# Four transformer layers on one core: layers 0 to 2 as one instruction sequence with one set of buffers

## The chip, the cores and the metric

The kernel runs on one core of a Trainium2 chip. Its engines work side by side, each through its own list of instructions, strictly in order: TensorE (PE, matrix products and transposes, with its weight loads shown as PEld), VectorE (DVE), ScalarE (ACT), GpSimd (POOL) and SyncE (SP, which here only issues DMAs). An instruction waits for semaphores that others raise, and whatever stands behind it on its engine waits too. The metric is the device time of one execution in microseconds; lower is better. The kernel before takes 1860.44 us, the median of three runs (1860.05 to 1869.56).

## The reference

The input x is 128 batches of 64 tokens with 128 channels, with a context of the same shape and one condition vector for each batch. Four layers follow one another:

```
L0: x = x + g_sa * (attend(ln(x)*(1+sc_sa)+sh_sa) @ sa_proj_w + b)     16 heads of 8
    x = x + attend(q from ln(x), k and v from context) @ ca_proj_w + b
    x = x + g_ff * (gelu((ln(x)*(1+sc_ff)+sh_ff) @ fc1_w + b1) @ fc2_w + b2)
L1: x = x + attend(q from ada_ln(x), k and v from ada_ln(context)) @ Wp + bp
L2: like L0, with ln(context) for its keys and values
L3: nx = layer_norm(x); evidence = softmax(nx Wq (ctx Wk)^T / sqrt(128)) ctx Wv
    combined = [nx, evidence, condition]
    x = x + sigmoid(gate(combined)) * (sum over 3 experts, by a softmax router, @ out_w + out_b)
```

The shifts, scales and gates of L0, L1 and L2 are products of silu(condition) with weights: small tables that are computed once. All is float32.

## The kernel before

The 8192 tokens are 16 groups of 512 (8 batches), and x stays in on-chip memory throughout (`xs`, one tile a group). The kernel is a row of stages, each a loop over the groups.

**Attention 1** is one pipeline of 32 items: L0's self-attention of 16 groups, then L0's cross-attention of 16. Each item is prepared in eight parts (`prepare`, L294): load of the context, statistics, norm, the transposed key and query inputs, `kT` and its masked copy `kbd` (L342, POOL), `qT`, and the values, written into one of two tiles `vbds`. Then come scores in two halves (`scores`, L365: maximum L382 and subtraction L384 on DVE), transposes and the exponential (`turned`, L390), the product with the values (`weighted`, L406), and `finish` (L427) in four parts: A sends the softmax sums to DRAM and back (L435 to L443); B takes reciprocals on DVE and sends them through DRAM into `rb`, spread over the rows (L445 to L457); C multiplies to `oT` and adds the bias to x on POOL (L460, L462); D projects on PE (`py`, L466) and adds to x on DVE. `attend` (L474) writes the order out by hand: first 8, 5, 3 and 2 parts of items 0 to 3, then steps k, two for an item, in which the parts of neighbouring items alternate. The last steps hold only finishes. For the last two items little else stands between the parts.

**Tables of later layers** (`later_layers`, L204): ten modulations, a folded column, a gate table that goes to DRAM, and two folded rows; each is one product on PE and one or two operations on DVE.

**MLP 0** (`mlp_loop`, L571): turn j holds the norm of group j+2 (POOL), the four hidden products of group j (`hidden`, L584, with Gelu on ACT, L585), the four output products of group j-1 (`output`, L590), the transposes and modulation of group j+1 (`enter`: DVE L258, POOL L259), the statistics of group j+3, the gate of j-1 and the residual of j-2 (`leave`, L602, L603). In each turn stands one group of `measure_context`: a load of the context and its statistics, with some POOL operations (L566 to L569), for the norms of L1 and L2.

**Attention 2** is the same pipeline over 48 items (L1 cross, L2 self, L2 cross). **Layer 3's setup** (L661 to L773) then loads its expert weights and multiplies weights with one another, each time a product on PE and a copy on DVE with two PSUM tiles. **MLP 2** follows, then **layer 3**.

Each of these stages opens its own pools of on-chip buffers and closes them at its end, so that the first loads of a stage wait for the end of the one before. The attention pools hold, in banks of PSUM, two `mm`, one `sc` of four and one `pt` of two; the MLP's hold three `mm`, three `ph` and two `py`. The order of the start (conditions, modulations, tables) is left to the scheduler; within the loops it is as written.

Of the kernel before, what the change touches and what calls it, by code (L numbers as in the profile page):

```python
# [59 lines left out]
def tile_kernel(ctx: ExitStack, tc: tile.TileContext, a: dict, out: bass.AP):  # L60
# [60 lines left out]


    masked = ExitStack()
    mp = masked.enter_context(tc.tile_pool(name="mp", bufs=1))
    dp = ctx.enter_context(tc.tile_pool(name="dp", bufs=1, space=bass.MemoryType.DRAM))
    vbds = []
    for i in range(2):
        t = mp.tile([P, NB, 8, 32], F32, tag=f"vbd{i}", name=f"vbd{i}")
        G.memset(t, 0.0)
        G.memset(t[0:L, :, :, 16:17], 1.0)  # L130
        G.memset(t[L:P, :, :, 17:18], 1.0)
        vbds.append(t)
# [14 lines left out]
    def modulations(ps0, *which):  # L147
        for wname, bname, n, scales in which:
            m = const([P, n, P], "mod_" + wname)
            for i in range(n):  # L150
                pm = ps0.tile([P, 512], F32, tag="ps", name="pm")
                T.matmul(pm[:, :P], w[wname][:, 0, ts(i, P)], scT, start=True, stop=True)
                r = _ROW[bname] + i
                b = (vec1 if i in scales else vec)[:, r : r + 1]
                V.tensor_scalar_add(m[:, i, :], pm[:, :P], b)
            mods[wname] = m
# [3 lines left out]
    def folded_column(ps0, wp, bp, bv, i):  # L160
        pb = ps0.tile([P, 512], F32, tag="ps", name="pb")
        T.matmul(pb[:, 0:1], w[wp][:, 0], col(bv, i), start=True, stop=True)
        t = const([P, 1], "pb_" + wp)
        V.tensor_add(t, pb[:, 0:1], col(bp))
        proj_bias[wp] = t
# [3 lines left out]
    def gate_table(ps0, wmod, wp):  # L169

        table = dp.tile([2, P, P], F32, tag="gate_" + wp, name="gate_" + wp)
        rows = const([P, 2, P], "gate_rows")
        gb = const([P, P], "gate_bias")
        V.tensor_scalar_mul(gb, mods[wmod][:, 2, :], proj_bias[wp])
        for i, src in enumerate((mods[wmod][:, 2, :], gb)):
            pg = ps0.tile([P, 512], F32, tag="ps", name="pg")
            T.transpose(pg[:, :P], src, ident)
            V.tensor_copy(rows[:, i, :], pg[:, :P])
        nc.sync.dma_start(table.rearrange("i b c -> b i c"), rows)
        gates[wp] = table  # L180

    def folded_row(ps0, wp, bp, bv):
        bvs = const([P, P], "bvs")
        V.tensor_copy(bvs, col(bv, 1).broadcast_to([P, P]))
        pb = ps0.tile([P, 512], F32, tag="ps", name="pb")
# [4 lines left out]
    with tc.tile_pool(name="ps0", bufs=2, space=PSUM) as ps0:  # L190
        pc = ps0.tile([P, 512], F32, tag="ps", name="pc")
# [3 lines left out]
        pv = ps0.tile([P, 512], F32, tag="ps", name="pv")  # L195
# [3 lines left out]
        modulations(ps0, ("L0_xcond_adaln_w", "L0_xcond_adaln_b", 6, (1, 4)))  # L199
        folded_column(ps0, "L0_xcond_sa_proj_w", "L0_xcond_sa_proj_b", "L0_xcond_qkv_b", 2)  # L200
        gate_table(ps0, "L0_xcond_adaln_w", "L0_xcond_sa_proj_w")
        folded_row(ps0, "L0_xcond_ca_proj_w", "L0_xcond_ca_proj_b", "L0_xcond_kv_b")

    def later_layers():  # L204
        with tc.tile_pool(name="ps0", bufs=4, space=PSUM) as ps0:
            modulations(
                ps0,
                ("L1_xcond_Wss_q", "L1_xcond_bss_q", 2, (0,)),
                ("L1_xcond_Wss_kv", "L1_xcond_bss_kv", 2, (0,)),
                ("L2_xcond_W_mod", "L2_xcond_b_mod", 6, (1, 4)),  # L210
            )
            folded_column(ps0, "L2_xcond_W_proj", "L2_xcond_b_proj", "L2_xcond_b_qkv", 2)
            gate_table(ps0, "L2_xcond_W_mod", "L2_xcond_W_proj")
            folded_row(ps0, "L1_xcond_Wp", "L1_xcond_bp", "L1_xcond_bkv")
            folded_row(ps0, "L2_xcond_W_cproj", "L2_xcond_b_cproj", "L2_xcond_b_kvc")
# [78 lines left out]
    def prepare(pools, at):  # L294
# [12 lines left out]
        if cross:  # L307
            cn = c
            if layer != "L0c":
                cn = pool.tile([P, TT, P], F32, tag="cn", name="cn")  # L310
# [116 lines left out]
    def finish(pools, at):  # L427
# [20 lines left out]
        rb = pool.tile([P, NT], F32, tag="rb", name="rb")  # L448
# [10 lines left out]
        oT = pool.tile([P, NT], F32, tag="oT", name="oT")  # L459
# [14 lines left out]
    def attend(pools, ats):  # L474
# [9 lines left out]
        for i, parts in enumerate((8, 5, 3, 2)):  # L484
            for _ in range(parts):
                go(prep, i)

        halves = [dict(at=at, u=u) for at in ats for u in range(2)]
        for k in range(2 * n + 6):
# [30 lines left out]

    def attention_of(s, layer):
# [29 lines left out]
    def mlp(wmod, w1, b1, w2, b2, beside=None):  # L551
        with ExitStack() as stack:
            pool = stack.enter_context(tc.tile_pool(name="wk", bufs=2))
            psum = stack.enter_context(tc.tile_pool(name="mm", bufs=3, space=PSUM))
            ph_pool = stack.enter_context(tc.tile_pool(name="ph", bufs=3, space=PSUM))
            py_pool = stack.enter_context(tc.tile_pool(name="py", bufs=2, space=PSUM))
            with tc.manual_schedule():
                mlp_loop(pool, psum, ph_pool, py_pool, wmod, w1, b1, w2, b2, beside)

    def measure_context(pool, s):  # L560
# [10 lines left out]
    def mlp_loop(pool, psum, ph_pool, py_pool, wmod, w1, b1, w2, b2, beside):  # L571
# [6 lines left out]
        def enter(d):  # L578
            d["xm"] = modulated(pool, transposed(psum, d["xn"]), wmod, 4, 3, d["s"])
            d["h"] = pool.tile([P, 4, NT], F32, tag="h", name="h")  # L580

        def hidden(d, f):
            ph = ph_pool.tile([P, 512], F32, tag="ph", name="ph")
# [3 lines left out]
        def output(d, f):  # L587
            if f == 0:
                d["py"] = py_pool.tile([P, 512], F32, tag="py", name="py")
# [21 lines left out]
        go(measure, 0)  # L611
        go(norm, 0)
        go(measure, 1)
        for j in range(-1, NST + 2):
# [9 lines left out]
            if beside and 0 <= j < NST:  # L624
                beside(pool, j)
# [5 lines left out]
    def attention_pools(stack):  # L631
        pool = stack.enter_context(tc.tile_pool(name="wk", bufs=2))
        psum = stack.enter_context(tc.tile_pool(name="mm", bufs=2, space=PSUM))
        psc = stack.enter_context(tc.tile_pool(name="sc", bufs=1, space=PSUM))
        ppt = stack.enter_context(tc.tile_pool(name="pt", bufs=1, space=PSUM))
        return pool, psum, psc, ppt
# [3 lines left out]

    with ExitStack() as stack:
        pools = attention_pools(stack)
        with tc.manual_schedule():
            attend(pools, [attention_of(s, layer) for layer in ("L0s", "L0c") for s in groups])
    later_layers()
    mlp(
        "L0_xcond_adaln_w", "L0_xcond_fc1_w", "L0_xcond_fc1_b", "L0_xcond_fc2_w", "L0_xcond_fc2_b",
        measure_context,
    )


    with ExitStack() as stack:
        pools = attention_pools(stack)
        with tc.manual_schedule():
            attend(
                pools, [attention_of(s, layer) for layer in ("L1c", "L2s", "L2c") for s in groups]
            )
    masked.close()


    keep = ctx.enter_context(tc.tile_pool(name="keep", bufs=1))  # L661
    load_weights("L3_xcond_e", keep)

    def kept(shape, name):
        return keep.tile(shape, F32, tag=name, name=name)

    g_b2 = kept([P, P], "g_b2")
    r = _ROW["L3_xcond_gate_b2"]
    nc.scalar.dma_start(g_b2, a["vecs"][r : r + 1, :].broadcast_to([P, P]))
    out_b = kept([1, P], "out_b")  # L670
    r = _ROW["L3_xcond_out_b"]
    nc.scalar.dma_start(out_b, a["vecs"][r : r + 1, :])

    r_b = kept([P, 1], "r_b")
    V.memset(r_b, 0.0)
    for t in range(TT):
        nc.scalar.dma_start(
            r_b[32 * t : 32 * t + 3, :], a["L3_xcond_router_b"].rearrange("(n o) -> n o", o=1)
        )
    three = kept([1, TT, 32], "three")  # L680
    V.memset(three, 0.0)
    V.memset(three[:, :, 0:3], 1.0)
    b2p = kept([P, TT, 32], "b2p")
    V.memset(b2p, 0.0)
    rw = kept([P, 3, 32], "rw")
    V.memset(rw, 0.0)
    V.tensor_copy(rw[:, 0, 0:3], w["L3_xcond_router_W"][:, 0, :])
    V.tensor_copy(rw[:, 2, 0:3], w["L3_xcond_router_W"][:, 2, :])
    w_qk = kept([P, P], "w_qk")
    w_ev = kept([P, 3, 256], "w_ev")  # L690
    w_gev = kept([P, P], "w_gev")
    w_2o = kept([P, 6, P], "w_2o")

    b_2o = kept([P, TT, P], "b_2o")
    V.memset(b_2o, 0.0)
    ab = kept([P, 7, P], "ab")
    ra = kept([P, NST, 2], "ra")
    pds, prs = [], []
    for i in range(2):
        t = kept([P, TT, P], f"pd{i}")  # L700
        G.memset(t, 0.0)
        pds.append(t)
        t = kept([P, TT, 32], f"pr{i}")
        G.memset(t, 0.0)
# [322 lines left out]
```

## Time and profile before

| view | row | value |
|---|---|---|
| runs | median of 3 | 1860.44 us |
| profiled execution | time, span | 1859.64, 1857.8 us |
| engines | PE busy | 1660.1 us (89%) |
| | DVE, ACT, POOL busy | 1250.0, 1082.8, 1031.6 us |
| timeline | first scores of attention 1 | 32.08 us |
| | last subtraction (L384) of attention 1 ends | 432.01 |
| | first hidden product of MLP 0 | 468.17 |
| | last hidden product of MLP 0 starts | 588.6 |
| | first scores of attention 2 | 614.11 |
| | last subtraction of attention 2 ends | 1234.75 |
| | layer 3's setup: first load issued | 1258.37 |
| | first hidden product of MLP 2 | 1291.62 |
| | last hidden product of MLP 2 starts | 1412.1 |
| DMA | share of the 16 engines, main queue | 17.9% |

The times in the table of the timeline are counted from the start of the span. A busy time is that of an engine's instructions; it says nothing of which engine the others wait for. In the lists of instructions the bracket at the end of a line gives how long the engine was idle before it, and on what it waited.

### The profile page before, as it was taken

What the parts mean: (1) busy time and instruction counts of PE and PEld (TensorE: products, weight loads), DVE (VectorE), ACT (ScalarE), POOL (GpSimd) and SP (SyncE); (2) the same over time, 40 slices, a digit from 0 to 9 for tenths busy, and PEclk for the clock granted to TensorE, in tenths of its full rate; (3) what the DMA queues carried; (4) which work ended last, traced back from release to release, by engine and by line L of the source; (5) the groups of instructions that cost most, each with busy time, mean ns of one, the idle gap of its engine ahead of it and who ended that gap; (6) DMA issues with size and microseconds to landing.
All of it is one profiled execution on the core that took longest, in us unless ns stands there. A gap on an engine that the chain in (4) does not pass through costs nothing.

```text
span 1857.8 us, 64728 instructions
## 1 busy us (share of the span) xinstructions
PE 1660.1 (89%) x27756; PEld 1103.7 (59%) x27756; DVE 1250.0 (67%) x2299; ACT 1082.8 (58%) x1862; POOL 1031.6 (56%) x1665
## 2 busy tenths in 40 slices
PE   5999889995998888899998899966997999999998
PEld 3666667764444566666666667753444566656665
DVE  4899889984453688899898899853342445444544
ACT  3877667772333787778777788841332444444443
POOL 5677777652996666666777667623552232223311
PEclk9999999998999899999999999985997999999999
DMA  6233332212111022212333322111000000000000
GB/s 185 57 86 89 93 94 68 68 45 59 30 34 34 24 58 55 53 44 60 79 89 89 103 68 68 51 51 36 1 1 17 23 18 18 24 23 24 18 7 17
DMA packets 149870, 95.79 MB, mean 52 GB/s; under 512 B 35221, under 2 KB 132431, under 8 KB 149583
## 3 DMA queue, kind: packets, MB, share of 16 engines
q1 hardware_dynamic: 148624, 91.35, 17.9%
q8 instruction: 218, 3.57, 0.8%
q14 instruction: 69, 0.57, 0.1%
q10 hardware_dynamic: 959, 0.30, 0.1%
HBM read 71.41 MB, written 9.70 MB: 44 GB/s over the span
## 4 chain that ended last, share of the span: by engine, by line
PE 55%; DMA 11%; DVE 10%; POOL 8%; issue 6%; ACT 5%; SPq 5%; POOLq 0%; ACTq 0%; DVEq 0%
PE ph L584 6%; PE py L590 6%; PE ph L904 5%; PE ph L905 5%; PE sc L375 5%; PE psT L253 5%; PE pp L400 4%; PE po L417 4%; DMA recs<-rc 3%; PE py L466 3%; DVE e L384 2%; DVE mx L382 2%; PE pk L334 2%; DMA rb<-recs 2%; PE pq L347 2%
## 5 line engine op out<-in xcount | busy, mean ns | idle before, releaser
L382 DVE TENSOR_REDUCE mx<-sc 128x32 f32<-128x2048 f32 x160 | 366.1, 2288 | 80.1 <-PE sc L375 80.0
L404 ACT ACTIVATE eT<-pp 128x1024 f32<-128x1024 f32 x320 | 330.3, 1032 | 103.2 <-PE pp L400 103.2
L384 DVE TENSOR_TENSOR e<-sc,mx 128x2048 f32<-128x2048 f32 x160 | 366.6, 2292 | 5.5
L400 PEld LDWEIGHTS pp<-ident,e 64*128 64x128 f32 x5120 | 184.8, 139 | 201.5 <-issue 80.4
L342 POOL TENSOR_SCALAR kbd<-kT,mask 128x512 f32<-128x512 f32 x320 | 216.1, 694 | 73.3 <-ACT kT L336 73.2
L400 PE MATMUL pp<-ident,e 64*128 64x64 f32 x5120 | 228.7, 229 | 20.7 <-ACT eT L404 15.6
L282 POOL TENSOR_SCALAR xn<-x,nmu,rs 128x128 f32<-128x128 f32 x512 | 223.5, 451 | 13.4
L375 PE MATMUL sc<-kbd,qT 32*64 32x256 f32 x5120 | 181.8, 391 | 23.3 <-DVE e L384 22.8
L460 POOL TENSOR_TENSOR oT<-o,rb 128x512 f32<-128x512 f32 x80 | 102.0, 1275 | 161.9 <-DMA rb<-recs 79.3
L585 ACT ACTIVATE h<-ph,vec 128x512 f32<-128x512 f32 x128 | 88.0, 688 | 173.2 <-PE ph L584 173.2
L907 DVE TENSOR_TENSOR h<-ph,ab 128x512 f32<-128x512 f32 x112 | 77.5, 692 | 157.0 <-PE ph L905 157.0
L417 PE MATMUL po<-eT,vbd 128*32 128x64 f32 x10240 | 177.0, 221 | 1.8 <-ACT eT L404 1.8
L240 POOL TENSOR_SCALAR rs<-mv 128x4 f32<-128x4 f32 x128 | 25.5, 199 | 246.1 <-DVE mv L233 202.4
L417 PEld LDWEIGHTS po<-eT,vbd 128*32 128x32 f32 x10240 | 150.7, 110 | 12.9 <-ACT eT L404 2.1
L241 POOL TENSOR_TENSOR rs<-rs,nhalf 128x4 f32<-128x4 f32 x128 | 130.3, 1018 | 10.7
L911 ACT ACTIVATE h<-h 128x512 f32<-128x512 f32 x112 | 70.4, 630 | 109.0 <-DVE h L907 90.1
L375 PEld LDWEIGHTS sc<-kbd,qT 32*64 32x64 f32 x5120 | 98.9, 132 | 58.9 <-issue 39.4
L336 ACT ACTIVATE kT<-pk,vec 128x512 f32<-128x512 f32 x80 | 55.1, 688 | 109.9 <-PE pk L334 109.9
L231 DVE BATCH_NORM_STATS2 st<-x 128x6 f32<-128x128 f32 x512 | 110.5, 278 | 8.4 <-DMA x<-in_x_dram 8.4
L936 PE MATMUL po<-w_2o,h 128*128 128x128 f32 x768 | 98.5, 278 | 19.1 <-DVE acc L946 18.4
L425 ACT COPY o<-po 128x512 f32<-128x512 f32 x160 | 95.6, 598 | 26.3 <-DMA gt<-gate_L_xcond_W_proj 6.2
L936 PEld LDWEIGHTS po<-w_2o,h 128*128 128x128 f32 x768 | 90.7, 192 | 24.8 <-issue 13.1
(259 smaller groups left out, 2997.2 us busy)
## 6 DMA issues: line engine op xcount, KB each, us to landing
rb<-recs SPq DMA_DIRECT2D x80, 256.0 KB
c<-in_ctx_dram SPq DMA_DIRECT2D x80, 256.0 KB
o<-o SPq DMA_DIRECT2D x320, 32.0 KB
gt<-gate_L_xcond_sa_proj_w SPq DMA_DIRECT2D x64, 128.0 KB
gt<-gate_L_xcond_W_proj SPq DMA_DIRECT2D x64, 128.0 KB
sums<-o SPq DMA_DIRECT2D x320, 8.0 KB
x<-in_x_dram SPq DMA_DIRECT2D x16, 256.0 KB
out_dram<-acc SPq DMA_DIRECT2D x16, 256.0 KB
```

What stands on the lines that cost most here:

```text
L241: G.tensor_tensor(rs, rs, nhalf, ALU.pow)
L282: G.tensor_scalar(xn[:, t, :], src[:, t, :], nmu[:, t : t + 1], rs[:, t : t + 1], ALU.add, ALU.mult)
L342: G.tensor_scalar(kbd[:, j], by_batch(kT), mask[:, j : j + 1], 1.0, ALU.mult, ALU.mult)
L375: T.matmul(sc[ts(h, L), g, ts(t2, 256)], qT[ts(g, 32), ts(b, L)], kbd[ts(g, 32), :, b, :], start=True, stop=True,)
L382: V.tensor_reduce(mx, sc.rearrange("p g (m k) -> p (g m) k", k=L), AX.X, ALU.max)
L384: V.tensor_tensor(e, sc.rearrange("p g (m k) -> p (g m) k", k=L), mx.unsqueeze(2).broadcast_to([P, 32, L]), ALU.subtract,)
L400: T.transpose(pp[:, h, ts(4 * g2 + 2 * i + t2, L)], e6[ts(h, L), 2 * gg + g2, t2, i], ident[ts(h, L), ts(h, L)],)
L404: S.activation(eT[:, gg], pp, AF.Exp, scale=HD ** -0.5)
L417: T.matmul(po[ts(g, 32), i, ts(2 * t2 + h, L)], at["vbd"][:, 4 * u + 2 * t2 + h, 2 * g + i, :], e7[:, g // 2, h, g % 2, i, t2, :], start=T ...
L584: T.matmul(ph, w[w1][:, 0, ts(f, P)], d["xm"], start=True, stop=True)
L590: T.matmul(d["py"], w[w2][:, f, :], d["h"][:, f, :], start=f == 0, stop=f == 3)
L936: T.matmul(po[:, ex, :], d[q][:, ts(t, P)], w_2o[:, q, :], start=r == 0, stop=r == 1)
```

## The change

Layers 0 to 2 become one sequence, written by hand from the first transposes on, with one set of pools (the attention's). `attend` and `mlp` no longer run their loops; they return lists of functions, and `stages` calls these in turn. The tail of an attention (its last four steps) alternates with the head of the MLP's loop (its first four turns, -1 to 2), and the last two turns of MLP 0 alternate with the three functions that prepare the first items of attention 2. The tables of later layers stand one by one in turns 0 to 8 of MLP 0, and layer 3's setup in turns 0 (loads and memsets) and 3 to 15 of MLP 2, joined into fewer PSUM tiles and copies. At the start, only two of L0's six modulations stand ahead of the first scores. `rb`, `oT` and `cn` have one buffer instead of two, the MLP's hidden tile takes the place of `e`, `ph` that of `sc` and `py` that of `pt`, and layer 3's kept tiles take the places of weights that are no longer needed. Layer 3's loop is the same.

```diff
+    pools = (
+        stack.enter_context(tc.tile_pool(name="wk", bufs=2)),
+        stack.enter_context(tc.tile_pool(name="mm", bufs=2, space=PSUM)),
+        stack.enter_context(tc.tile_pool(name="sc", bufs=1, space=PSUM)),
+        stack.enter_context(tc.tile_pool(name="pt", bufs=1, space=PSUM)),
+    )
...
-    def modulations(ps0, *which):
+    def modulations(wname, bname, n, scales):
+        def part(which):
+            pm = mm("pm")
+            for j, i in enumerate(which):
+                T.matmul(pm[:, ts(j, P)], w[wname][:, 0, ts(i, P)], scT, start=True, stop=True)
+            for j, i in enumerate(which):
...
+                V.tensor_scalar_add(mods[wname][:, i, :], pm[:, ts(j, P)], b)
+        return [lambda q=q: part(range(q, min(q + 2, n))) for q in range(0, n, 2)]
...
+    later_tables = [
+        *modulations("L1_xcond_Wss_kv", "L1_xcond_bss_kv", 2, (0,)),
+        *modulations("L1_xcond_Wss_q", "L1_xcond_bss_q", 2, (0,)),
+        *modulations("L2_xcond_W_mod", "L2_xcond_b_mod", 6, (1, 4)),
+        lambda: folded_row("L1_xcond_Wp", "L1_xcond_bp", "L1_xcond_bkv"),
+        lambda: folded_column("L2_xcond_W_proj", "L2_xcond_b_proj", "L2_xcond_b_qkv", 2),
+        lambda: gate_table("L2_xcond_W_mod", "L2_xcond_W_proj"),
+        lambda: folded_row("L2_xcond_W_cproj", "L2_xcond_b_cproj", "L2_xcond_b_kvc"),
+    ]
...
-                cn = pool.tile([P, TT, P], F32, tag="cn", name="cn")
+                cn = pool.tile([P, TT, P], F32, tag="cn", name="cn", bufs=1)
-        rb = pool.tile([P, NT], F32, tag="rb", name="rb")
+        rb = pool.tile([P, NT], F32, tag="rb", name="rb", bufs=1)
-        oT = pool.tile([P, NT], F32, tag="oT", name="oT")
+        oT = pool.tile([P, NT], F32, tag="oT", name="oT", bufs=1)
...
-        for i, parts in enumerate((8, 5, 3, 2)):
-            for _ in range(parts):
-                go(prep, i)
+        heads = [
+            lambda: ahead(0, 1, 2, 0, 1, 0, 1),
+            lambda: ahead(0, 0, 0, 0, 0),
+            lambda: ahead(2, 1, 1, 2, 3, 3),
+        ]
...
+        return heads, [lambda k=k: step(k) for k in range(2 * n + 5)]
...
-            d["h"] = pool.tile([P, 4, NT], F32, tag="h", name="h")
+            d["h"] = pool.tile([P, 4, NT], F32, tag="e", name="h")
-            ph = ph_pool.tile([P, 512], F32, tag="ph", name="ph")
+            if f == 0:
+                d["ph"] = psc.tile([P, 4, 512], F32, tag="sc", name="ph")
+            ph = d["ph"][:, f]
...
+                if not pys:
+                    pys.append(ppt.tile([P, 2, 512], F32, tag="pt", name="py"))
+                d["py"] = pys[0][:, d["s"] % 2]
...
+        def head():
+            go(measure, 0)
+            go(norm, 0)
+            go(measure, 1)
...
-            if beside and 0 <= j < NST:
-                beside(pool, j)
+            if 0 <= j < NST:
+                beside(j)
...
+        return head, [lambda j=j: turn(j) for j in range(-1, NST + 2)]
...
+    def l3_loads():
...
+        k3["raw1"] = pool.tile([P, 6, 256], F32, tag="kbd", name="raw1")
+        for ex in range(3):
+            nc.sync.dma_start(k3["raw1"][:, 2 * ex : 2 * ex + 2], e_w1[:, ex, 1:3])
...
+    def l3_evidence(exs):
+        p = mm("ps")
+        for i, ex in enumerate(exs):
+            T.matmul(
+                p[:, ts(i, 256)], k3["wT"][:, 2], k3["raw1"][:, 2 * ex, :], start=True, stop=True
+            )
+        for i, ex in enumerate(exs):
+            V.tensor_copy(k3["w_ev"][:, ex, :], p[:, ts(i, 256)])
...
+    l3_parts = [
+        l3_loads, l3_turned, l3_small, lambda: l3_evidence((0, 1)), lambda: l3_evidence((2,)),
+        lambda: l3_second((0, 1, 2, 3), 0), lambda: l3_second((0, 1, 2, 3), 1),
+        lambda: l3_second((4, 5), 0), lambda: l3_second((4, 5), 1), l3_bias,
+        lambda: l3_anchor((0, 1)), lambda: l3_anchor((2, 3)), lambda: l3_anchor((4, 5, 6)),
+        l3_router,
+    ]
...
+        def beside_0(j):
+            measure_context(j)
+            if j < len(later_tables):
+                later_tables[j]()
+        def beside_2(j):
+            if j == 0 or 0 < j - 2 < len(l3_parts):
+                l3_parts[max(j - 2, 0)]()
...
+        last = 4
+        def side_by_side(xs_, ys_):
+            for i in range(max(len(xs_), len(ys_))):
+                for z in (xs_, ys_):
+                    if i < len(z):
+                        z[i]()
+        condition()
+        clear(vbds[0])
+        first[0]()
+        clear(vbds[1])
+        first_mods[0]()
+        first[1]()
+        first[2]()
+        steps_1[0]()
+        first_mods[1]()
+        first_mods[2]()
+        first_tables()
+        for f in steps_1[1:-last]:
+            f()
+        head_0()
+        side_by_side(steps_1[-last:], turns_0[:last])
+        for f in turns_0[last:-2]:
+            f()
+        side_by_side(second, turns_0[-2:])
+        for f in steps_2[:-last]:
+            f()
+        head_2()
+        side_by_side(steps_2[-last:], turns_2[:last])
+        for f in turns_2[last:]:
+            f()
```

`first` and `second` are the `heads` of the two attentions, `turns_0` and `turns_2` the turns of the two MLPs, each list starting at turn -1.

## What was predicted

> **What bounds the kernel now.** I read the 40 slices first, to see the stages; then busy times by stretch, cut where a line starts or ends; then the timeline at each cut, for the wait that ends last there.
>
> ```profile
> PE   5999889995998888899998899966997999999998
> POOL 5677777652996666666777667623552232223311
> PEclk9999999998999899999999999985997999999999
> ```
>
> A slice is 46.4 us. TensorE dips at the start and in slices 11, 24, 28 to 29 and 31: the joins between attention and MLP, and of layers 2 and 3. Inside stages it is full or paced by another engine, so the question is what each join costs. The stretches (columns: from:to, length, then busy us and instruction count of PE, PEld, DVE, ACT, POOL, then granted clock, DMA share, GB/s):
>
> ```profile
> 0.00:32.00 32.00, 14.37 (x64) 8.67 (x64) 8.67 (x48) 6.57 (x14) 14.32 (x33) 0.99 0.94 254
> 432.00:468.00 36.00, 15.54 (x216) 12.98 (x216) 11.39 (x48) 4.50 (x5) 14.65 (x21) 0.72 0.19 53
> 481.00:560.00 79.00, 79.00 (x242) 38.70 (x242) 41.06 (x190) 27.65 (x41) 71.60 (x152) 1.00 0.12 34
> 590.00:617.00 27.00, 18.11 (x106) 8.98 (x105) 8.98 (x40) 12.30 (x32) 11.89 (x22) 0.71 0.17 49
> 1230.00:1258.00 28.00, 12.57 (x284) 11.09 (x280) 6.88 (x6) 5.83 (x7) 7.48 (x6) 0.67 0.17 47
> 1258.00:1292.00 34.00, 18.96 (x67) 12.21 (x66) 15.11 (x68) 1.28 (x1) 8.83 (x21) 0.55 0.18 48
> 1305.00:1384.00 79.00, 79.00 (x245) 38.98 (x244) 30.89 (x110) 28.20 (x41) 43.14 (x83) 1.00 0.00 1
> ```
>
> In the joins every engine is half idle and the clock is cold (0.55 to 0.72): latency chains, one after the other. In the MLP stretches PE is at 79.00 of 79.00. What stands in the joins, by the timeline:
>
> ```profile
> 450.77 1.26 POOL L460 TENSOR_TENSOR oT<-o,rb 128x512 f32<-128x512 f32 x1 [7.07 <-DMA rb<-recs]
> 452.09 2.08 PE L466 MATMUL py<-L_xcond_ca_proj_w,oT 128*128 128x128 f32 x8 [7.48 <-POOL oT L460]
> 460.37 0.20 POOL L240 TENSOR_SCALAR rs<-mv 128x4 f32<-128x4 f32 x1 [7.11 <-PE pg L177]
> 1267.04 2.93 PE L730 MATMUL ps<-L_xcond_e_w,wvT 128*128 128x256 f32 x6 [5.45 <-DMA L_xcond_e_w<-in_L_xcond_e_w_dram]
> 1291.62 2.08 PE L584 MATMUL ph<-xm,L_xcond_W_mlp 128*128 128x512 f32 x2 [3.94 <-POOL xm L259]
> ```
>
> The last group's softmax sums go to DRAM and back before POOL and PE can finish it (7 us waits); tables or layer 3's weights follow (5.45 us for their DMA); only then does the MLP's first norm start.
>
> **Join 1, attention to MLP 0.** After the change the MLP's head and turns -1 to 2 stand between the last four attention steps. DVE is free for the head once the reciprocal of group 14 ends (timeline: 435.70 + 0.54 = 436.24). One group's stats on DVE (0.86 + 0.36) end at 437.5. From there POOL works in order, with the durations that it shows from 460.37 on: rs 1.2, nmu and xn 2.05, second rs 1.2, group 14's oT and x+bias 2.55 (its rb landed at 441.2), second norm 2.05, add for xm 1.05: 447.6. The first hidden matmul can go at about 447.8, not at its 468.17. This isn't all gain, since in MLP 0 POOL paces:
>
> ```profile
> 556.36 0.20 POOL L279 TENSOR_SCALAR nmu<-mv 128x4 f32<-128x4 f32 x1
> 564.22 0.19 POOL L279 TENSOR_SCALAR nmu<-mv 128x4 f32<-128x4 f32 x1
> ```
>
> POOL needs 7.86 us a turn, PE 7.74 (hidden matmuls of successive turns at 575.20 and 582.94). So I count on POOL. It goes from rs at 460.37 to the third xm at 480.8 without a gap: 20.4. After: 437.6 + 20.4 + 5.1 (the tail's two oT and x+bias, now in between) = 463.1 for turn 2, against 481.1. From there PE: 13 turns x 7.74 = 100.6, plus the tables that now stand in turns. A table part is 4 passes of 128 columns; psB's four take 0.43 warm at issue, and I add about 0.15 for weight loads: seven parts from turn 2 on, 3.7. Turn 15 then starts at 567.4, was 582.94: **15.5 us**. Behind the tail's reciprocal on DVE (waits to about 445) stand turn 0's operations on DVE; they aren't late, since POOL's queue ends later. Three more context loads pass SP after the tail's last rb issue, so they delay no finish. Bounds: 10 if each table costs a PE-DVE exchange, 20 if PE absorbs them.
>
> **Join 2, MLP 0 to attention.** Heads go among the last two turns. In the timeline before, stats follow the last residual add (596.59 + 0.69 = 597.28) and scores come at 614.11. Now they come right behind the gate of group 14 (ends 591.9): first stats end at 593.2. POOL: rs twice, nmu and xn twice (6.4), to 599.6. ACT: cn(0) is done early, but cn(1) now stands ahead of cm(0) and, with its single buffer, behind cn(0)'s transposes on PE (after the outputs of group 15, about 594); 1.65 for it, 2.48 for cm(0): 598.6. pk on PE is 2.07 cold plus xn's transposes, kT 0.69: 601.6. kbd 2.70: 604.3. qT and pvv end in the same microsecond; scores at about 605.5: **9 us** (bounds 4, if cn(1) waits longer, to 11).
>
> **Join 3, attention to MLP 2.** The same count from the reciprocal's end (1240.2): stats 1241.5, POOL rs, xn, rs to 1246.2, oT and x+bias 1248.8, second norm 1250.8, add 1251.9. First hidden at 1251.9, was 1291.62. Turn 2 stood 14.24 later before (cold clock and ramp); with group 15's py (1.1, half beside waits) it is at 1267. POOL has ten memsets of layer 3 (2.9) ahead of group 15's oT, and reaches xm(2) at 1266: not late. SP's thirteen layer 3 loads stand behind the tail's last DMA and have three turns (23 us) to land, against 8.54 on the chain now. Layer 3's setup moves into turns 3 to 15 of a PE that is full, so its PE time stays: about 20 transposes at 0.11, 19 products of two passes at 0.215, three at 0.43, the small ones 0.3: 6.4 at warm issue rate, plus 13 x 0.15: 8.3. DVE's copies (some 6 us) lie beside, DVE being busy 30.89 of 79. Turn 15: 1267 + 100.6 + 8.3 = 1375.9, was 1406.54: **31 us** (bounds 24 to 37, as PE's setup costs 15 or 3).
>
> The clock in this sum: the Trainium skill, "TensorE: Matmul & The Clock Gate", Part 1, has the array at half clock until some 3.4 us of activity. By its rule a join's end costs about 1.7; by the row, turns 0 and 1 took 14.24 against 4.3 + 7.7 = 12.0 warm, so 2.2. I kept the row's, so I claim no gain by a warmer start.
>
> **Start.** Four of the six modulations and the gate table go behind the first scores, and the second vbd's clearing behind two norms. Stats of group 1 end on DVE at 10.1 as now (its x lands at 8.98). POOL: rs twice to 11.5, xn(0) 13.5; the two modulations that xm needs are done by 11. Then as now from psT on: transposes, ACT's eight xm 2.48 to 16.5; pk, kT to 19.4; kbd 22.1; pvv and group 1's transposes; scores about 23.4, now 32.08. But the tables then stand on DVE between first and second softmax half, and PE waits for them: second mx at about 35.3, now 40.18: **5 us** (bounds 1 to 8).
>
> **Buffers.** rb, oT and cn go from two buffers to one. The skill ("Trainium Kernel Development and Optimization", Best Practices) says to double-buffer so that DMA overlaps compute; that speaks against this. The rows:
>
> ```profile
> 712.28 1.28 POOL L460 TENSOR_TENSOR oT<-o,rb 128x512 f32<-128x512 f32 x1
> 720.57 0.55 SPq L449 DMA_DIRECT2D rb<-recs  x1
> ```
>
> The reader ends at 713.56, the next write is issued 7.0 later. oT has 11.6 (py's end to the next oT); cn 2.5 (717.07 to 719.56). By the rule, serialising DMA and product would add rb's 4 us a group, x 80 = 320; by the rows, 0. I take the rows. The MLP's PSUM shrinks too: psT, setup and psB share two slots (were three for two); each slot is wanted again a third to half a turn after its fill, about 2.5 us, against 0.69 for DVE's read. Hidden's four banks keep bank-wise waits: gelu of part 3 ends 0.4 before the next turn. I take 0, and 0 to 0.5 a turn (16) for the range.
>
> **Sum.** 15.5 + 9 + 31 + 5 = 60.5. The profiled execution took 1859.64 with a span of 1857.8: 1799.1 for it. The median of the three runs shown is 0.8 above: **1800**. Layer 3 and the steady turns of attention are left as they are.
>
> **Rivals.**
> A. Only the setup leaves the path; in-order queues still wait out the tail's DRAM trips, since each engine's tail instruction blocks the turns behind it. For it: DVE's reciprocal and PE's py do stand ahead of turn work. Against: turns need nothing of groups 14 and 15, and only POOL's and PE's waits of some 2 us fall where no turn work is ahead. Then join 1 gives its tables' stretch less their PE time (455.0 to 461.5, 6.5 - 3.7 = 2.8), join 3 its setup's (1258.4 to 1286.4, 28 - 8.3 = 19.7), with 9 and 5: 36.5, so 1824.
> B. More is hidden: setup falls into PE's gaps, MLP 0 isn't paced by POOL: join 1 gives 20, join 3 37, join 2 11: about 1785. Against it: PE has no gaps in 481 to 560.
> C. Slower: the two shared PSUM slots act as one. Each of three fills a turn would wait for its forerunner's read (0.69 + about 0.2): 2.7 x 28 turns = 76, so 1876. It decides from 60.5 / 28 = 2.2 us a turn. For it: DVE has up to 5 us a turn in MLP 0, in order, so a read can lag behind stats. Against: a lag of a third of a turn is free.
> D. The change doesn't do what it says: the listed order of the built program has turns between tail steps on all engines, so I give it almost nothing.
>
> **Chances.** Forecast 0.68 (1788 to 1815), A 0.18, B 0.10, C and the like 0.04. The range 1784 to 1825 takes in B and most of A. 0.5% (9 us) is about what a measurement of this kernel can tell from no change. Faster 0.96, same 0.02, slower 0.02.
>
> **What would show it.** First scores near 23; first hidden of MLP 0 near 448 less the start's gain; gap from last hidden of MLP 0 to first scores some 9 shorter; first hidden of MLP 2 within 23 us of attention's last softmax, PE near full from its third turn; turns of 7.7 to 8.4 us; SP's rb issues waiting for no POOL. Wrong would be: PE waits named after DVE reads of psT or psB; POOL idle in MLP 0; attention groups slower than 11.9 to 14.1 us apart.

## The result, and the profile after

The changed kernel takes **1840.5 us** (median of four runs, 1837.66 to 1841.48), against 1860.93 for the kernel before in the same comparison: a ratio of 0.9877, with a 95% interval of 0.9846 to 0.9909. It is faster, by some 20 us and not by 60, and above the predicted range of 1784 to 1825. The profiled execution took 1840.96 with a span of 1839.2.

The page of the kernel after, 40 slices of 46.0 us:

```profile
PE   5999889997999788899998999978996999999998
POOL 5687676755876666667776776646432233223311
PEclk9999989998999999999999999999998999999999
```

The dips at the joins that follow the attentions have shrunk: from 5 to 7 in the 10th slice (join 1), from 6 and 6 to 7 and 8 in the 27th and 28th (join 3). The clock no longer falls to 5 at join 3. So these joins did close. Slice 31, at MLP 2's end, went from 7 to 6. The stretches of the two MLPs, at the same places as before (columns as there):

```profile
481.00:560.00 79.00, 73.76 (x225) 33.01 (x224) 38.82 (x175) 24.05 (x35) 62.50 (x131) 1.00 0.11 31
1305.00:1384.00 79.00, 74.35 (x243) 35.63 (x243) 28.59 (x89) 23.37 (x34) 30.42 (x58) 1.00 0.00 1
```

Here PE had 79.00 of 79.00. Now it has 5 us of holes in each, and POOL and ACT do less in the same time: the turns have become longer. The first and last hidden product of each MLP, from the view of the tile ph (count, then shortest/median/longest in ns, then first and last start in us):

```profile
L604 PE MATMUL ph<-xm,L_xcond_fc_w x128: 592/594/1223, 447.5 to 588.8; 128*128 128x512 f32 x128
L604 PE MATMUL ph<-xm,L_xcond_W_mlp x128: 592/593/1223, 1245.2 to 1390.8; 128*128 128x512 f32 x128
```

With these, and with the first and last score products of the timeline, the span falls into eight stretches. The column "waits removed" is the last experiment below:

| stretch, us | before | after | waits removed | predicted change |
|---|---|---|---|---|
| start to last scores of attention 1 | 426.2 | 424.8 | 422.7 | -5 |
| to the first hidden of MLP 0 | 42.0 | 22.7 | 21.4 | -20.4 |
| first to last hidden of MLP 0 | 120.4 | **141.3** | 124.0 | +4.9 |
| to the first scores of attention 2 | 25.5 | 19.0 | 19.1 | -9 |
| first to last scores of attention 2 | 614.8 | 614.4 | 618.3 | 0 |
| to the first hidden of MLP 2 | 62.7 | 23.0 | 22.8 | -39.7 |
| first to last hidden of MLP 2 | 120.5 | **145.6** | 128.3 | +8.7 |
| to the end | 445.7 | 448.4 | 445.6 | 0 |
| span | 1857.8 | 1839.2 | 1802.2 | -60.5 |

("Scores" are counted by the start of their first and of their last row in the timeline. The predicted changes are those of the steps, with a join's net gain split at its first hidden product: 468.17 - 447.8 = 20.4, of which 15.5 was to be left at turn 15, so MLP 0 was to grow by 4.9; likewise 39.7 and 31 at join 3.) The joins gave 19.3, 6.5 and 39.7. The two MLPs took back 20.9 and 25.1, where 4.9 and 8.7 had been allowed. One plain turn of MLP 0, without a setup part, shows it. The timeline, with the lines of PE, of PE's weight loads and of one gate:

```profile
564.02 1.02 PE L604 MATMUL ph<-xm,L_xcond_fc_w 128*128 128x512 f32 x2
564.82 0.75 DVE L616 SCALAR_TENSOR_TENSOR y<-py,vec,mod_L_xcond_adaln_w 128x512 f32<-128x512 f32 x1
565.62 1.12 PE L612 MATMUL py<-h,L_xcond_fc_w 128*128 128x512 f32 x2 [0.58 <-DVE y L616]
...
567.88 1.02 PE L612 MATMUL py<-h,L_xcond_fc_w 128*128 128x512 f32 x2
568.09 0.69 ACT L605 ACTIVATE h<-ph,vec 128x512 f32<-128x512 f32 x1 [2.32 <-PE ph L604]
568.82 0.30 PEld L604 LDWEIGHTS ph<-xm,L_xcond_fc_w 128*128 128x128 f32 x2 [0.75 <-ACT h L605]
568.83 1.13 PE L604 MATMUL ph<-xm,L_xcond_fc_w 128*128 128x512 f32 x2
569.79 1.02 PE L612 MATMUL py<-h,L_xcond_fc_w 128*128 128x512 f32 x2
...
574.59 0.70 PE L612 MATMUL py<-h,L_xcond_fc_w 128*128 128x512 f32 x1 [0.58 <-DVE y L616]
```

The same place in a turn of the kernel before, in its MLP 2:

```profile
1336.83 1.02 PE L584 MATMUL ph<-xm,L_xcond_W_mlp 128*128 128x512 f32 x2
1337.64 0.75 DVE L594 SCALAR_TENSOR_TENSOR y<-py,vec,mod_L_xcond_W_mod 128x512 f32<-128x512 f32 x1
1337.69 1.02 PE L590 MATMUL py<-h,L_xcond_W_mlp 128*128 128x512 f32 x2
```

There the output product starts 0.86 after the hidden one, while the gate still runs.

In the change, the turn is 574.59 - 565.62 = 8.97, where PE's own work is 7.74. Two waits stand in it.

- The first output product of a turn starts at 565.62, when the gate has ended (564.82 + 0.75). That gate reads the *other* half of py. Start to start, this gap is 1.60 where a product takes 0.86: 0.74 lost. The product after it comes 0.97 later, not 0.86: another 0.11.
- Hidden slice 2 starts at 568.83, when the gelu of slice 1 has ended (568.09 + 0.69). That gelu reads *another bank* of ph. The gap is 0.95, and the next 0.96: 0.19 lost. Slice 3 loses as much.

Together 0.85 + 0.37 = 1.22 a turn. In 15 turns of two MLPs that is 37 us, by this estimate: somewhat more than the 32 that is missing (20.9 + 25.1 less 4.9 + 8.7).

### The profile page after: what moved, and what is told of

It reads as the page before. It is cut to its first block, busy times and chain, and to the rows that moved or that the text cites. A ratio compares the mean times of both kernels' runs of the same rounds, so it can differ in the third digit from the quotient of the medians.

```text
span 1839.2 us, 64747 instructions
## 1 busy us (share of the span) xinstructions
PE 1661.5 (90%) x27756; PEld 1090.1 (59%) x27756; DVE 1247.4 (68%) x2281; ACT 1082.4 (59%) x1862; POOL 1032.8 (56%) x1671
## 5 line engine op out<-in xcount | busy, mean ns | idle before, releaser
L254 POOL TENSOR_SCALAR rs<-mv 128x4 f32<-128x4 f32 x128 | 25.5, 199 | 230.6 <-DVE mv L247 190.4
```

## The experiments

Three theories stood after this reading. **Theory 1**: the waits follow the tile as the program declares it, not the bank; py and ph were made tiles of two and four banks, each with readers and writers in flight. **Theory 2**, rival C of the prediction: the two shared slots of psT, psB and setup hold the turns up. **Theory 3**: setup parts cost far more in a turn than their PE time. Ratios are to the kernel before, run beside each; differences between kernels are taken from the ratios, at 1861 us. The diffs are cut to the lines that matter.

**Gate ahead of leave.**

```diff
-            go(leave, j - 2)
             go(gate, j - 1)
+            go(leave, j - 2)
```

> The changed kernel with gate(j-1) put ahead of leave(j-2) at the end of a turn. Theory 1, tile-wide waits: the first output of a turn waits for the gate just issued, although that gate reads the other half of the shared py tile; with the gate first on VectorE it ends 0.75 us earlier, and the wait (0.74, and 0.11 of restart, in some 30 turns) goes: about 1815 us, plain MLP turns near 8.1 instead of 8.97. Theory 2, the two shared PSUM slots of psT, psB and setup hold the turns up: psB's read comes later now, so not faster, 1840 or more. Theory 3, the setup parts' exchanges between TensorE and VectorE cost the time: no change, 1840.

1812.31 us, ratio 0.9757 (0.9735 to 0.9778): 22 less than the change. Its turn in the timeline:

```profile
556.51 1.02 PE L604 MATMUL ph<-xm,L_xcond_fc_w 128*128 128x512 f32 x2
557.38 1.02 PE L612 MATMUL py<-h,L_xcond_fc_w 128*128 128x512 f32 x2
...
564.63 1.02 PE L604 MATMUL ph<-xm,L_xcond_fc_w 128*128 128x512 f32 x2
565.50 1.02 PE L612 MATMUL py<-h,L_xcond_fc_w 128*128 128x512 f32 x2
```

The output follows its hidden product after 0.87, with no wait named, and the turn is 8.12: 0.85 gone, as theory 1 had it. Theory 2 has psB read later here, and no plain turn got longer for it. (In the profiled execution turns 0 and 1 of MLP 2 did, 11.50 and 10.99 against 9.38 and 8.64, at a granted clock of 0.63 from 1222 to 1245, where the change had 0.87 from 1245 to 1263. MLP 0 got 10.8 shorter, MLP 2 only 6.4.) The wait on the gate was an order on VectorE that two swapped lines mend.

**One two-bank py in the kernel before**, with nothing else of the change.

```diff
-                d["py"] = py_pool.tile([P, 512], F32, tag="py", name="py")
+                if not pys:
+                    pys.append(py_pool.tile([P, 2, 512], F32, tag="py", name="py", bufs=1))
+                d["py"] = pys[0][:, d["s"] % 2]
```

> The kernel before, with the one part of the change that makes MLP's py one tile of two banks, its halves used in turn; nothing else. Theory 1: each first output of a turn waits for the gate of the other half: 0.85 us in some 30 turns, 26 more: about 1886. Theories 2 and 3: no change, 1861.

1881.35 us, ratio 1.013 (1.0109 to 1.015): 24 more. py takes two banks in both versions, one a turn in alternation; only the declaration differs, and the wait is there. In its timeline:

```profile
561.45 1.12 PE L592 MATMUL py<-h,L_xcond_fc_w 128*128 128x512 f32 x2 [0.58 <-DVE y L596]
...
570.05 1.12 PE L592 MATMUL py<-h,L_xcond_fc_w 128*128 128x512 f32 x2 [0.58 <-DVE y L596]
```

The same 0.58 at the same place, and a turn of 8.60 = 7.74 + 0.86.

**Transposes two and two**: half of psT's and of psB's transposes in each of the four gaps between hidden products, so that each gap is 0.86 + 0.22, longer than the 0.94 that a gelu needs.

```diff
-            go(enter, j + 1)
+            go(turn_in, j + 1, 0)
             go(hidden, j, 1)
             go(output, j - 1, 1)
+            go(enter, j + 1)
...
                 beside(j)
+            go(turn_out, j - 2, 0)
             go(hidden, j, 3)
```

> The changed kernel with the four transposes of psT and of psB set two and two into the four gaps between a turn's hidden products. Theory 1: hidden slice f waits for the gelu of slice f-1, although that reads another bank of the same tile; the gap that this leaves to one output product (0.86) is short of the 0.94 that the gelu needs, and two more transposes (0.22) fill it: 0.37 us a turn less, some 12 in all, about 1828. Theory 2: psT and psB hold their slots about a microsecond longer, so slower, up to 1870. Theory 3: no change, 1840.

1832.94 us, ratio 0.9858 (0.983 to 0.9886): 3.5 less, not 12, and the interval overlaps that of the change. Plain turns did lose their 0.37 (544.07 to 552.67, psB to psB: 8.60). But three table parts of MLP 0, whose PE input comes from VectorE, now stood behind psT's later read there, and PE waited 1.43 for each; the next run shows the same. Turn 0 of MLP 0 went from 8.89 to 10.12, and the turns of MLP 2 that hold a setup part lost only 0.2.

**Both edits.**

> Both edits: gate ahead of leave, and transposes two and two. Theory 1: both waits go, plain turns 7.75 to 7.9, about 1803. Theory 2: 1840 or slower. Theory 3: 1840.

1808.6 us, ratio 0.9738 (0.9718 to 0.9758). Plain turns are 7.78. One of the three table parts in the timeline:

```profile
493.06 0.20 DVE L198 COPY bvs<-vec 128x128 f32<-128x128 f32 x1
493.40 0.46 PE L200 MATMUL pb<-L_xcond_Wp,bvs 128*128 128x128 f32 x2 [1.43 <-DVE bvs L198]
```

Mending one wait by moving work across a queue made another. A variant avoids it: psB's halves a gap earlier, with leave there, and psT's first half at the end of the turn before.

> Both waits taken away without the cost that the run with both edits showed (three table parts of MLP 0 whose input comes from VectorE stood behind psT's later read, 1.4 us of TensorE wait each): gate last on VectorE's queue but leave earlier, psB's halves in gaps 2 and 3, psT's first half at the end of the turn before. Theory 1: plain turns 7.75, the three long turns gone, 5 us less than with both edits: about 1803. Theory 2: psT's slot is now held over a turn's end, so shared slots would bind here most: 1815 or more.

1805.2 us, ratio 0.9731 (0.9709 to 0.9752). The 1.43 waits are gone, but by the ratio it can't be told from the run with both edits: turn 0 has no output products to fill its gaps, so its hidden products still wait for whole gelus. In MLP 0 it takes 7.69 from its second hidden product to the first output (448.29 to 455.98), against 4.61 (446.81 to 451.42) in the last experiment below, where ph is four tiles.

**Four one-bank tiles for ph.** At each MLP the pool of scores is closed and a pool of four tiles opened on its four banks (`own` does both).

```diff
-            if f == 0:
-                d["ph"] = psc.tile([P, 4, 512], F32, tag="sc", name="ph")
-            ph = d["ph"][:, f]
+            if not swapped:
+                own("ph", 4)
+                swapped.append(1)
+            ph = psc[0].tile([P, 512], F32, tag="ph", name="ph")
```

> The changed kernel, with the four-bank pool of scores closed ahead of each MLP's first hidden product and a pool of four one-bank ph tiles opened in its place, nothing else. Theory 1: hidden slice f then waits for its own bank's gelu of a turn ago: 0.37 us a turn less, 12 in all, about 1828; first outputs still wait for the gate. Theory 2: no change, 1840. Swapping the pool may itself cost a microsecond at each of three places.

1822.35 us, ratio 0.9814 (0.9798 to 0.9831): 12 less than the change, as expected. The timeline:

```profile
545.36 1.02 PE L625 MATMUL py<-h,L_xcond_fc_w 128*128 128x512 f32 x2
546.22 1.02 PE L617 MATMUL ph<-xm,L_xcond_fc_w 128*128 128x512 f32 x2
547.08 1.02 PE L625 MATMUL py<-h,L_xcond_fc_w 128*128 128x512 f32 x2
```

Gaps of 0.86, although the gelus are no faster and the banks are the same. The wait on the gate stays (turn 8.60).

**Fewer slots in the kernel before**: psT and psB share two slots instead of three; then, in a second run, ph as one tile of four banks as well.

> The kernel before, with the one part of the change that leaves MLP two PSUM slots for psT and psB instead of three. Theory 1: no change, 1859. Theory 2 (the shared slots act as one): a wait of 0.9 at two fills a turn, 58 us more: 1917; setup parts aren't in it.

> The kernel before, with two slots for psT and psB and hidden's four slices in one tile of four banks instead of three tiles of one bank. Theory 1: 0.37 us a turn more than the run with two slots alone, 12 in all: 1871. Theory 2: nothing more than the run with two slots.

The first: 1858.79 us, ratio 1.0004 (0.9991 to 1.0018). **Theory 2 falls**: two slots cost nothing for psT and psB. (Setup's parts, which share the slots in the change, aren't in this run; in the last run below they are, and PE is full.) The second: 1879.61, ratio 1.0119 (1.0102 to 1.0137), 21 more than two slots alone, where 12 were expected. Its turns are 8.12, as expected; the rest is turn 0, which I had left out. It has no output products between its hidden ones, so each waits for a whole gelu:

```profile
472.60 1.44 PE L586 MATMUL ph<-xm,L_xcond_fc_w 128*128 128x512 f32 x2
474.82 1.12 PE L586 MATMUL ph<-xm,L_xcond_fc_w 128*128 128x512 f32 x2 [0.78 <-ACT h L587]
476.72 1.12 PE L586 MATMUL ph<-xm,L_xcond_fc_w 128*128 128x512 f32 x2 [0.78 <-ACT h L587]
478.72 1.10 PE L586 MATMUL ph<-xm,L_xcond_fc_w 128*128 128x512 f32 x2 [0.87 <-ACT h L587]
479.65 1.02 PE L592 MATMUL py<-h,L_xcond_fc_w 128*128 128x512 f32 x2
```

From turn 0's second hidden product to the first output it takes 7.05 (472.60 to 479.65), against 3.95 with two slots alone (473.96 to 477.91): 3.1 in MLP 0. In MLP 2 it is 7.52 against 3.70. Together that is 7 of the 9 that were missing.

**Joins in sequence**: all of the stage that ends, then the head and turns of the next.

```diff
-            for i in range(max(len(xs_), len(ys_))):
-                for z in (xs_, ys_):
-                    if i < len(z):
-                        z[i]()
+            for f in (*xs_, *ys_):
+                f()
...
```

> The changed kernel without alternation: at each of the three joins all remaining steps of the stage that ends come first, then the head and the turns (or steps) of the next; buffers, spread setup and the first two softmax halves' order stay. Prediction: the part of the joins' gain that is not the setup's, 12.7 at join 1, 9 at join 2, 11.3 at join 3, goes: some 33 more, 1873. Rival A (in-order queues wait out the tail anyway, only the setup left the path): 0 to 10 more, 1840 to 1850.

1877.81 us, ratio 1.0072 (1.0048 to 1.0096): 36 more than the change, 33 expected. From attention's last scores to the first hidden product it takes 40.1 and 40.0 (22.7 and 23.0 in the change), and 25.2 at join 2 (19.0). At join 1 PE stands through the tail's trip to DRAM first, then through the norm:

```profile
448.08 2.07 PE L480 MATMUL py<-L_xcond_ca_proj_w,oT 128*128 128x128 f32 x8 [7.89 <-POOL oT L474]
454.19 1.77 PE L267 MATMUL psT<-ident,xn 128*128 128x128 f32 x4 [4.03 <-POOL xn L296]
459.87 2.07 PE L604 MATMUL ph<-xm,L_xcond_fc_w 128*128 128x512 f32 x2 [3.91 <-POOL xm L273]
```

Rival A of the prediction falls: taking alternation away costs 36, where by it at most 10 was expected, and putting the setup back in a row (the next run) costs 14.

**Setup in a row**: tables ahead of MLP 0, layer 3's parts after MLP 2.

```diff
-            if j < len(later_tables):
-                later_tables[j]()
...
+        for f in later_tables:
+            f()
         head_0()
...
+        for f in l3_parts[1:]:
+            f()
```

> The changed kernel with the setup parts in a row: the tables of layers 1 and 2 ahead of MLP 0's head, layer 3's parts (loads apart) after MLP 2's last turn; alternation stays. Prediction: the two rows come back on the path, about 6.5 and 22 (28 less the 5.45 for weights that are there by now), and turns lose what the parts cost in them, 5.0 in MLP 2 and 0.7 in MLP 0 by the turns of the changed kernel: 20 more, 1860. Rival: the parts cost in the turns what they cost in a row: no change, 1840.

1853.31 us, ratio 0.9951 (0.9934 to 0.9968): 14 more than the change, not 20. It is also the measure of what setup costs inside turns: without it the MLPs are 140.1 and 140.2 long, so in the change the parts add 1.2 and 5.4. Theory 3 falls: 6.6 of the 46 are setup. The rest, 19.7 in each MLP (140.1 - 120.4, 140.2 - 120.5), is the waits and whatever the alternation adds to the first turns. Directly, **the waits cost 17.3 in each MLP of the change**: that is what the last run below takes off (141.3 - 124.0, 145.6 - 128.3).

**Two buffers for rb** (`bufs=1` taken off its line).

> The changed kernel with rb back at two buffers, nothing else. Prediction (single buffers cost nothing, the next write being issued 7 us after the reader's end): no change, 1840, ratio 0.988. Rival (layer 0's self-attention, 403 us from first to last scores after the change against 394 before, is longer because rb's load waits for its buffer): some 5 us less, 1835, ratio 0.985, and that stretch back near 395.

1840.69 us, ratio 0.9887 (0.9865 to 0.9909), and attention 1's scores take 400.4, inside the scatter of the versions with one buffer (395.7 to 404.3). No gain from the second buffer can be told; oT and cn weren't tried.

**Both waits away**: gate ahead of leave, and four one-bank ph tiles; no transpose is moved.

> The changed kernel with gate ahead of leave and four one-bank ph tiles: both waits taken away with no transposes moved. Theory 1: the two gains add up, 22.5 + 11.7 us as measured one at a time: ratio 0.9694, about 1804; plain turns 7.75. If the two waits cover each other: no better than 0.9757, the ratio of the gate alone.

1804.18 us, **ratio 0.9688 (0.967 to 0.9706)**: the two gains add up, and it is the best version here. Its windows have PE at the full length again, as in the first line below, and a plain turn is 7.75 (538.87 to 546.61, psB to psB):

```profile
481.00:560.00 79.00, 79.00 (x254) 39.41 (x253) 41.64 (x186) 27.68 (x41) 71.25 (x150) 1.00 0.13 36
...
538.87 0.60 PE L637 MATMUL psB<-ident,y 128*128 128x128 f32 x4
539.31 1.02 PE L617 MATMUL ph<-xm,L_xcond_fc_w 128*128 128x512 f32 x2
540.17 1.02 PE L625 MATMUL py<-h,L_xcond_fc_w 128*128 128x512 f32 x2
541.02 0.60 PE L279 MATMUL psT<-ident,xn 128*128 128x128 f32 x4
...
546.61 0.60 PE L637 MATMUL psB<-ident,y 128*128 128x128 f32 x4
```

## Why the prediction was wrong, step by step

**The step that failed is "Buffers": "Hidden's four banks keep bank-wise waits ... I take 0, and 0 to 0.5 a turn (16) for the range."** The runs put 1.22 a plain turn in its place, and 35 us in all: the ratio fell from 0.9877 to 0.9688 when both waits were taken away. The waits go by the declared tile: two banks of one tile are not independent of each other. I priced the slots that got fewer (psT and psB, for which no cost can be told: ratio 1.0004) and took for granted that separate banks mean separate waits. Of py's new form I said nothing, and it costs more than twice as much a turn as ph's: 0.85 against 0.37. The diff showed both (`d["ph"][:, f]`, `pys[0][:, d["s"] % 2]`), and the trace of before had the rows to price them: a gate of 0.75 issued at the end of a turn, and a gelu that ends 0.89 after the start of the output product (in MLP 0, 572.38 + 0.69 against 572.18), where that product covers 0.86. There the next hidden product could start before the gelu's end; in one tile it could not. The range's 16 was reached by guess, not from these rows. The sign that I named, "PE waits named after DVE reads of psT or psB", pointed at the wrong tile: they are named after DVE's y and ACT's h. Another sign, "POOL idle in MLP 0", did come (62.50 busy of 79, against 71.60 before, and 71.25 again once the waits are gone): it followed from the longer turns.

The other terms, by the stretches of the table:

- **Join 1** held: first hidden 19.3 sooner of 20.4. MLP 0, with the waits removed, grows by 3.6 of 4.9. The step says that POOL paces MLP 0 at 7.86 a turn, yet its sum charges 13 turns at 7.74. The 7.74 was a misreading there: 582.94 is a weight load, and the hidden product of that turn starts at 583.05, so that turn took 7.85. It is right for MLP 2. Nor does POOL need 7.86: that is the spacing of its rows, of which it was busy for 7.13. Without the waits a plain turn takes 7.75, with POOL busy for 7.02. What made it 7.86 in the kernel before was not tried.
- **Join 2** was 6.5 of 9, inside its bounds of 4 to 11.
- **Join 3** was 39.7 of 39.7 to the first hidden product. Setup in MLP 2 and the slower start cost 7.8 of 8.7, once the waits are gone. Here two errors met: the terms listed for setup add up to 7.9 (20 x 0.11 + 19 x 0.215 + 3 x 0.43 + 0.3), not 6.4, and with 13 x 0.15 to 9.8, not 8.3; turns 3 to 14 showed 7.0.
- **Setup's PE time** showed as 6.6 in the change, against 12.0 estimated; with the waits removed the MLPs are 11.4 longer than before. Two costs overlap: a part stands in the third gap, and fills the time in which hidden slice 3 would have waited for a gelu. In MLP 2 of the change:

```profile
1334.67 0.38 PE L758 MATMUL ps<-ident,raw 128*128 128x128 f32 x2
1334.88 1.02 PE L604 MATMUL ph<-xm,L_xcond_W_mlp 128*128 128x512 f32 x2
1335.75 1.02 PE L612 MATMUL py<-h,L_xcond_W_mlp 128*128 128x512 f32 x2
```

  The product after slice 3 comes 0.87 later, so slice 3 did not wait, and this turn is only 0.03 longer than a plain one (9.00 against 8.97). Over turns 3 to 14 of MLP 2 the parts add 4.8 in the change and 7.0 in the kernel without the waits (to 7.75 a turn). The difference is 0.18 a turn: slice 3's share.
- **Start**: first scores came at 21.74, predicted 23.4; the second reduction of scores came at 35.09, predicted 35.3, before 40.18. In the profiled execution the rest of attention 1 took 3.8 of this back: the last scores came 1.3 sooner. Over ten executions of versions of the changed kernel they came at 422.3 on average, against 426.4 in four of versions of the kernel before: 4.1 sooner. In one execution this term is lost in scatter (see the end).
- **Rival C** named the right stage and the right kind of loss, a wait in each turn, but the wrong tile. Its price of 2.7 a turn is more than twice the 1.22 measured.
- **Reading the page**: the dips of the kernel before are in slices 10, 27, 28 and 31, not 11, 24, 28 to 29 and 31. The stretches were cut by times, so nothing in the sum hangs on it.

With the one term corrected the sum stands: 1799.1 was predicted for the profiled execution, and the kernel without the two waits took 1803.97. In no stretch of the table is it off by more than 3.5.

## What to carry to other kernels

When PSUM is pooled into fewer, larger tiles, count the tiles, not the banks: as in these runs, each write to a tile may wait for the last read issued on any part of it, so price that read's end against the next write's start, in program order, for every pair in a turn. Declare what is filled and drained in turn as separate tiles, or put the read first on its engine's queue. And price a turn without its usual cover too: the first turn of a pipeline has nothing between the products that wait.

## What the runs showed of the chip

A wait on TensorE costs more than its length: after a waiting product of an MLP the next one starts 0.96 later in most places here, not 0.86 (569.79 after 568.83, 0.97 in 566.59 after 565.62). The weight load of the waiting product starts with it (568.82 for 568.83); in the output product before, which does not wait, it starts 0.42 ahead (567.46 for 567.88). A wait of 0.08 thus costs 0.18.

Layer 0's attention scatters more after the change: first to last scores took 395.7 to 404.3 in ten executions of versions of the changed kernel, 394.1 to 395.5 in four of versions of the kernel before. Some 6 of the length are the tables that now stand between the first two softmax halves (12.13 between their reductions in the change, 5.98 before). The width, 8.6 against 1.4, isn't. From one item to the next it takes 12.1 to 17.7 us in the second half of self-attention and at the start of cross-attention, in both kernels, and which items are long differs from execution to execution. POOL's oT waits there for rb or gt by DMA, up to 4.5 in versions of the changed kernel, but up to 4.2 in versions of the kernel before too. The run with a second buffer for rb, at 400.4, lies in the middle of the range. With four executions of the one against ten of the other, the cause of the width stays open.
